# One logarithm over three PSUM banks in a pairwise-attention layer, and 128-column row transforms in a spectral layer

## The chip, the cores and the metric

The kernel runs on one core of one Trainium2 chip, in one launch. A core has five engines that each work through their own queue in order: TensorE (PE in the profile, with its weight loads as PEld), VectorE (DVE), ScalarE (ACT), GpSimd (POOL) and SyncE (SP, which here only issues DMAs). The metric is the device time of one launch in microseconds (us), and lower is better. The kernel before took 3248.14 us (median of 4 runs, 3234.2 to 3256.91).

## The reference

The input x is (4, 32, 128, 128) in float32: four batches of 32 images of 128 x 128 pixels. Two layers follow each other.

Layer 0 is an attention over the 32 images of a batch whose projections are spectral convolutions. Cut to what matters here:

```
x  = x + L0(group_norm(x))
L0: k, q, v = spectral convolutions with 32 heads of the normed images
    p  = spectral convolution of softmax(q k / 64) v;   a = inorm(p + images)
    m  = two spectral convolutions of inorm(a), a gelu between them
    result = inorm(m) + a
spectral convolution: rfft2, keep some modes, multiply by complex weights, irfft2
```

Layer 1 takes each of the four batches as 4096 tokens of 128 channels (32 blocks of 128 tokens). It is an additive attention over all earlier tokens, and a top-2 mixture of 8 experts:

```
f, g   = x W1[:h], x W1[h:]                       # 16 numbers per token
scores = sum_a w2[a] tanh(f_i + g_j + b1)[a] + b2  # for each pair i, j
e      = exp(scores) where j < i, else 0
w      = e / sum(e);   t = t + w x                 # then experts: t = t + sum of the best 2 of 8
```

## The kernel before, in words

**Layer 0.** The two-dimensional transform of an image is two matrix products. `forward` takes eight images at a time (`GI = 8`). In its first half each image, as the stationary operand of TensorE, meets the constant `rows`, whose 192 columns are cos, -sin and -cos of 64 frequencies. Two images fill a PSUM tile `pz` (2 x 192 columns, tag "a", two buffers), and one call of `evacuate` copies it to `z` in SBUF. Over its calls `evacuate` goes round in threes: two go to ScalarE, one to VectorE. In the second half each image of `z` is the stationary operand of two products, with columns 0 to 127 and with columns 64 to 191, which add up in PSUM tile `px` (tag "b"); `take` then reads `px`. A float32 product is two passes in the profile, each with its own weight load. `forward` is called for four groups of eight images by three users in each of four batches: for the images themselves (`spectra_of_images`, tiles named x), for `q` and for `g` (the two calls of `spectra`). That is 48 calls, 384 products into `pz` and 768 passes. `inverse` uses the same tags "a" and "b", and the same `evacuate`. The order of the instructions in layer 0 is made by a scheduler that sees the dependencies.

**Layer 1.** The tanh of a sum is made out of products: `prepare` turns each token into exponentials `qe`, `qf` (as a query) and `ke`, `kf` (as a key) over 2^6, 2^5 and 2^5 sign patterns, so that the score of a pair is a sum over three groups of a numerator `n` over a denominator `d`, each a matrix product with 32 rows to a tile; four such products use different rows of TensorE side by side. The work is cut into 528 units, one for 128 keys by 512 queries (the last of a row is put together out of smaller parts). Each turn `u` of the main loop issues

- `products(u)`: the denominators of unit u and the numerators of unit u - 1, ordered so that both run side by side;
- the logarithm of the denominators on ScalarE, `r = ln(d)`;
- for unit u - 1, whose r is already 1/d, the product n times r on VectorE and two additions on GpSimd that sum the three groups into the score `e`;
- the exponential of -r on ScalarE, in place (which makes 1/d of unit u), and that of the score of unit u - 2;
- `attend(u - 4)`: the product of e with the tokens into `po`.

After these, small pieces of other work, out of lists written by `prepare` and `finish` (norms, transposes, exponentials of keys and queries, the router, the experts `px`), are put in by a rule that counts what each costs. So layer 1's order is fixed by the program (`manual_schedule`). PSUM has eight banks in layer 1, one buffer each: `d0` two, `d1` one, `n0` two, `n1` one, `po` one, and `misc` one. The dictionary `PARTS` says which groups lie in which tile. A tile has to be read before it is written again: the first product of the next unit into `d0` waits for the logarithm of `d0`. After the main loop, `misc` rotates over the freed banks too (list `banks`).

Lines that the text speaks of: `forward` 266 to 283 (products 274, 281 and 282), `evacuate` 215 to 221, `PARTS` 1263, products of the units 1293, logarithm 1346, exp(-r) 1358, exp of the score 1362, product with n 1351, additions 1354 and 1355, `po` 1312, experts 1181 (their sums 1185), `pa` 1121, transposes `pt` 1061, keys and queries 1078 and 1089, router 1159.

Of the kernel before, what the change touches and what calls it, by code (L numbers as in the profile page):

```python
# [7 lines left out]
F32 = mybir.dt.float32  # L8
AF = mybir.ActivationFunctionType
ALU = mybir.AluOpType  # L10
# [3 lines left out]
P = 128  # L14
# [4 lines left out]
GI = 8  # L19
# [16 lines left out]
def _constants():  # L36

    w = np.arange(P)
    kx = np.concatenate([np.arange(32), np.arange(-32, 0)])
    ky = np.arange(KY)  # L40
    th = 2 * np.pi / P
    c, s = np.cos(th * np.outer(w, kx)), np.sin(th * np.outer(w, kx))
    rows = np.concatenate([c, -s, -c], 1)
    inv_rows = np.concatenate([c.T, -s.T], 0)
    angle = th * np.outer(w, ky)
    cc, cs = np.cos(angle), np.sin(angle)

    cols1 = np.concatenate([cc[:, 32:33], cs, cc, -cs], 1) / NPIX
    cols2 = np.concatenate([0 * cc[:, :1], -cc, cs, cc], 1) / NPIX
    twice = np.where(ky == 0, 1.0, 2.0)[:, None]  # L50
    re, im = twice * cc.T, -twice * cs.T
    inv_cols = np.concatenate([re, im], 0)
    p = np.arange(P)
    same = (p[:, None] % 32 == np.arange(32)[None, :]).astype(np.float64)
    block = (p[:, None] // 32 == np.arange(4)[None, :]).astype(np.float64)

    eye = np.eye(32)
    comb = np.zeros((4, 32, 3, 32))
    comb[0, :, 0], comb[3, :, 0] = eye, -eye
    comb[1, :, 1], comb[2, :, 1] = eye, eye  # L60
    comb[:, :, 2] = -comb[:, :, 0]
    halves = np.concatenate([np.eye(64), np.eye(64)], 0)

    group = (p[:, None] // 4 == p[None, :] // 4) / (4.0 * NPIX / C * T)
    of_group = p[:, None] // 4 == np.arange(32)[None, :]
    by_p = np.concatenate(
        [rows, inv_rows, cols1, cols2, same, block, comb.reshape(P, 96), halves, group, of_group / 4],
        1,
    )
    return by_p.astype(np.float32), inv_cols.astype(np.float32)  # L70


NX = 1 + 3 * KY
NCONST = 192 + 128 + 2 * NX + 32 + 4 + 96 + 64 + P + 32
NM = KX * KY
NK = 13

# [27 lines left out]
def layer0(  # L105
    tc, x, kcw, qcw, vcw, pcw, m0cw, m1cw, mcol0, heads, small_row, by_p, inv_cols, dram, x1
):
    nc = tc.nc
    pools = [tc.tile_pool(name="l0_const", bufs=1), tc.tile_pool(name="l0_ps", bufs=2, space=PSUM)]
    pools.append(tc.tile_pool(name="l0_x", bufs=2))  # L110
    const, ps, images = (p.__enter__() for p in pools)
# [17 lines left out]
    def columns(n):  # L129
        at[0] += n  # L130
        return cst[:, at[0] - n : at[0]]

    rows = columns(192)
    inv = columns(128)
    cols1, cols2 = columns(NX), columns(NX)
    same, block = columns(32), columns(4)
# [75 lines left out]

    flip = [0]

    def evacuate(out, in_):

        flip[0] = (flip[0] + 1) % 3
        if flip[0]:
            nc.scalar.copy(out, in_)
        else:  # L220
            nc.vector.tensor_copy(out, in_)

    def per_image(name):
        return small.tile([P, T], F32, name=name, tag=name)
# [41 lines left out]
    def forward(images, c1, c2, take, change=None):  # L266


        n = c1.shape[1]
        z = grp.tile([P, GI, 192], F32, name="z", tag="z")  # L270
        for k in range(0, GI, 2):
            pz = ps.tile([P, 2, 192], F32, name="pz", tag="a")
            for j in range(2):
                nc.tensor.matmul(pz[:, j], images[k + j], rows, start=True, stop=True)  # L274
            evacuate(z[:, k : k + 2], pz)
        if change is not None:
            change(z)
        for k in range(0, GI, 4):
            px = ps.tile([P, 4, n], F32, name="px", tag="b")
            for j in range(4):  # L280
                nc.tensor.matmul(px[:, j], z[:, k + j, :P], c1, start=True, stop=False)  # L281
                nc.tensor.matmul(px[:, j], z[:, k + j, 64:], c2, start=False, stop=True)  # L282
            take(k, px)
# [139 lines left out]
    for part, (a, b, c, d, op) in enumerate(  # L423
# [13 lines left out]
        for y0 in range(0, KA, 16):  # L437
            n = min(16, KA - y0)
# [188 lines left out]
    for b in range(B):  # L627
# [63 lines left out]
        for x0 in range(0, KX, NK):  # L691
# [3 lines left out]
            for i in range(4):  # L695
                xb = late.tile([P, 2, NK * KY], F32, name="xb", tag="xb")[:, :, :m]
                for r in range(2):
                    nc.sync.dma_start(
                        out=xb[:, r],
                        in_=xd[8 * i : 8 * i + 8, r, x0 : x0 + nk]  # L700
# [7 lines left out]
                for k in range(2):  # L708
                    for ri in range(2):
# [6 lines left out]
                        for r in range(2):  # L716
                            j = 2 * ri + r
# [12 lines left out]
        for y0 in range(0, KY, 8):  # L730
            n = min(8, KY - y0)
# [154 lines left out]
        for g in GROUPS:  # L886
            i = slice(g, g + GI)
            for t in range(g, g + GI):
# [5 lines left out]
                    scale=c2[:, t : t + 1],  # L894
# [17 lines left out]
def layer1(tc, x1, w1t_in, signs, vec17, expert_w, expert_b, router_w, small_row, out):  # L912
    nc = tc.nc
# [8 lines left out]
    const, keys, work, small, ps = (p.__enter__() for p in pools)  # L922
# [16 lines left out]
        out=later,  # L939
        in_=later,  # L940
# [15 lines left out]
    banks = ["m"]  # L956

    def misc(name):
# [9 lines left out]
        out=eb.rearrange("p e c -> p (e c)"),  # L968
        in_=expert_b.rearrange("e c -> (e c)").partition_broadcast(P),
    )  # L970
    for w, row in (
# [4 lines left out]
        n = w.shape[1]  # L976
# [283 lines left out]

    PARTS = {"d": (slice(0, 2), slice(2, 3)), "n": (slice(1, 3), slice(0, 1))}

    def two_parts(name):
        return [
# [72 lines left out]
    with tc.manual_schedule():  # L1339
        for u in range(len(units) + 4):  # L1340
            products(u)
            if u < len(units):
                r = work.tile([P, 3, QC], F32, name="r", tag="r", bufs=3)
                live[u, "r"] = r
                for g, d in zip(PARTS["d"], live.pop((u, "d"))):
                    nc.scalar.activation(r[:, g], d, AF.Ln, scale=1.0 / DSCALE)  # L1346
            if 0 <= u - 1 < len(units):
                v = u - 1
                r, n = live.pop((v, "r")), live.pop((v, "n"))
                for g, part in zip(PARTS["n"], n):  # L1350
                    nc.vector.tensor_tensor(r[:, g], part, r[:, g], ALU.mult)  # L1351
                e = work.tile([P, QC], F32, name="e", tag="e", bufs=5)
                live[v, "e"] = e
                nc.gpsimd.tensor_tensor(e, r[:, 1], r[:, 2], ALU.add)  # L1354
                nc.gpsimd.tensor_tensor(e, e, r[:, 0], ALU.add)  # L1355
            if u < len(units):
                r = live[u, "r"]
                nc.scalar.activation(r, r, AF.Exp, scale=-1.0)  # L1358
            if 0 <= u - 2 < len(units):
                c, h, _, parts = units[u - 2]  # L1360
                e = live[u - 2, "e"]
                nc.scalar.activation(e, e, AF.Exp)  # L1362
                if parts[0][0] >= chunks[c][1] + h * QB:

                    width = 2 * P if parts[-1][1] != h else P
                    own = e[:, : len(parts) * width].rearrange("p (k c) -> p k c", c=width)[:, :, :P]
                    nc.gpsimd.tensor_tensor(own, own, later[:, : len(parts)], ALU.mult)  # L1367
            if 0 <= u - 4 < len(units):
                attend(u - 4)
                c, h, is_last, _ = units[u - 4]  # L1370
                if is_last and c == len(chunks) - 1:
                    b, i0 = chunks[c]
                    ending.append((b, i0 + h * QB, QB, [sums[c, h]]))
                elif is_last and h == 1:
                    ending.append((*chunks[c], NB, [sums[c, h] for h in range(2)]))

            if starts and u >= starts[0][0] and not todo:
                _, c, end = starts.pop(0)
                todo = sum(begin(c), [])
            if ending and (not ended or len(ended) == 1 and len(ended[0]) <= 2 * NB):  # L1380
                ended.append(finish(*ending.pop(0)))
            hurry = sum(p[0] in (SOME, LATER) for p in todo) + 6 > end - u
            queues = sorted(ended, key=lambda p: len(p) <= 2 * NB)
            queues.insert(0 if hurry else 2, todo)
            pe, dve, pool = False, 0.0, 0.0
            for pieces in queues:
                while pieces:
                    kind, t_dve, t_pool, piece = pieces[0]
                    if kind == LATER:
                        pieces.pop(0)  # L1390
                        break
                    if kind and pe or dve + t_dve > 1.8 or pool and pool + t_pool > 1.7:
                        break
                    if kind in (SOME, KEEPS) and keeper and keeper[0] is not pieces:
                        break
                    pe, dve, pool = pe or kind > 0, dve + t_dve, pool + t_pool
                    if kind in (KEEPS, KEPT):
                        keeper = [pieces] if kind == KEEPS else []
                    pieces.pop(0)
                    piece()  # L1400
            ended = [p for p in ended if p]

        banks += ["n1", "d1", "n0", "d0"]
        while ended and len(ended[-1]) > 2 * NB:
            ended[0 if len(ended) > 1 and ended[0] else -1].pop(0)[-1]()
        ended.insert(0, finish(*ending.pop(0), last=True))
        while ended:
            for pieces in ended:
                pieces.pop(0)[-1]()
                while pieces and pieces[0][0] in (LATER, KEPT):  # L1410
                    pieces.pop(0)[-1]()
            ended = [p for p in ended if p]
# [69 lines left out]
```

## Time and profile before

| what | value |
|---|---|
| median of 4 runs | 3248.14 us (3234.2 to 3256.91) |
| profiled execution, its own time | 3248.24 us |
| its span in the profile | 3246.4 us |
| mean granted TensorE clock | 0.968 |
| TensorE busy | 2995.8 us (92%) |
| VectorE, ScalarE busy | 2324.0 us and 2327.8 us (72% each) |
| GpSimd busy | 2141.4 us (66%) |
| layer 0 | about 0 to 1160 us |
| layer 1, main loop | about 1160 to 3183 us |
| layer 1, after the loop | about 3183 to 3246 us |

Times in the profile are microseconds from the start of the span. "Idle before, releaser" says how long an engine stood still before a group of instructions, and which instruction's end let it go on. Matmul ends are modelled, and passes overlap, so the distance between the starts of two passes says more than their length.

### The profile page before, as it was taken

To read this page: it belongs to the slowest core of one execution; us is meant where nothing else is said; L and a number is where in the kernel's file an instruction comes from. 1 tells how busy PE (TensorE), PEld (TensorE's weight loads), DVE (VectorE), ACT (ScalarE), POOL (GpSimd) and SP (SyncE) were. 2 spreads that over 40 slices of the span, in tenths; PEclk is the share of its full clock that TensorE was granted. 3 is DMA by queue.
4 is the path that set the end of the run, shared out by engine and by line. 5 is a ranking of instruction groups with operands and counts; after the bars stand their busy time and mean duration, and the time that the engine had idled before them with its cause. 6 is when DMAs were issued, how large, how long until landed. Compare 5 with 4: busy or idle time off the path is not lost.

```text
span 3246.4 us, 53386 instructions
## 1 busy us (share of the span) xinstructions
PE 2995.8 (92%) x19732; PEld 1579.8 (49%) x19732; DVE 2324.0 (72%) x5070; ACT 2327.8 (72%) x3205; POOL 2141.4 (66%) x1883
## 2 busy tenths in 40 slices
PE   6899899899898789999998999998999999999997
PEld 4278458548657634433444444444344434344443
DVE  6776777777676456777765868876677777687787
ACT  2244354354353469999998999998999999899992
POOL 1631551460461259978789887979878889888773
PEclk9899899999999779999999999999999999999998
DMA  4410420330230111010110010011100010101000
GB/s 106 110 34 1 100 71 1 50 121 1 29 116 1 52 47 30 1 37 7 30 37 24 1 36 14 8 30 30 30 16 22 14 36 24 36 1 30 14 14 13
DMA packets 150854, 111.67 MB, mean 34 GB/s; under 512 B 35871, under 2 KB 139394, under 8 KB 149986
## 3 DMA queue, kind: packets, MB, share of 16 engines
q1 hardware_dynamic: 133873, 102.42, 12.6%
q10 hardware_dynamic: 16720, 5.84, 0.8%
q8 instruction: 156, 2.56, 0.3%
q14 instruction: 105, 0.85, 0.1%
HBM read 67.26 MB, written 20.00 MB: 27 GB/s over the span
## 4 chain that ended last, share of the span: by engine, by line
PE 64%; POOL 11%; ACT 9%; DVE 8%; issue 6%; DMA 2%; ACTq 0%; POOLq 0%; DVEq 0%; SPq 0%
PE d L1293 18%; PE po L1312 10%; PE px L1181 6%; ACT r L1346 4%; PE po L718 4%; PE pz L274 4%; PE n L1293 3%; POOL e L1355 3%; PE four L296 3%; POOL e L1354 3%; PE pv L291 3%; PE px L282 2%; PE px L281 2%; ACT e L1362 2%; DVE r L1351 2%
## 5 line engine op out<-in xcount | busy, mean ns | idle before, releaser
L1351 DVE TENSOR_TENSOR r<-n,r 128x1024 f32<-128x1024 f32 (+1 forms) x1056 | 962.0, 953 | 478.6 <-PE n L1293 390.9
L1354 POOL TENSOR_TENSOR e<-r 128x512 f32<-128x512 f32 x528 | 674.0, 1277 | 268.2 <-DVE r L1351 267.5
L1346 ACT ACTIVATE r<-d 128x1024 f32<-128x1024 f32 (+1 forms) x1056 | 793.5, 803 | 64.2 <-PE n L1293 56.7
L1358 ACT ACTIVATE r<-r 128x1536 f32<-128x1536 f32 x528 | 783.5, 1484 | 16.7
L1355 POOL TENSOR_TENSOR e<-e,r 128x512 f32<-128x512 f32 x528 | 672.0, 1273 | 41.4
L1293 PE MATMUL d<-qe,ke 32*128 32x512 f32 (+3 forms) x2304 | 607.8, 602 | 38.2 <-ACT r L1346 36.3
L1312 PE MATMUL po<-e,kx 128*128 128x512 f32 (+3 forms) x1152 | 594.3, 605 | 17.5 <-POOL e L1367 17.5
L1293 PE MATMUL n<-qe,ke 32*128 32x512 f32 (+3 forms) x2304 | 605.2, 601 | 0.0
L1293 PE MATMUL d<-qf,kf 32*128 32x512 f32 (+3 forms) x2304 | 552.4, 554 | 0.0
L1293 PE MATMUL n<-qf,kf 32*128 32x512 f32 (+3 forms) x2304 | 552.2, 554 | 0.0
L1185 DVE SCALAR_TENSOR_TENSOR xc<-px,wgt,xc 128x128 f32<-128x128 f32 x1024 | 358.3, 350 | 43.6 <-PE px L1181 11.1
L1362 ACT ACTIVATE e<-e 128x512 f32<-128x512 f32 x528 | 325.8, 617 | 67.6 <-POOL e L1355 66.6
L1312 PEld LDWEIGHTS po<-e,kx 128*128 128x128 f32 x1152 | 175.4, 188 | 394.2 <-issue 308.7
L1293 PEld LDWEIGHTS d<-qe,ke 32*128 32x128 f32 x2304 | 177.2, 183 | 359.8 <-ACT r L1346 340.7
L800 POOL TENSOR_TENSOR spec<-spec,part 128x264 f32<-128x264 f32 x64 | 55.6, 868 | 391.3 <-DVE part L797 188.7
L713 POOL TENSOR_TENSOR u<-xb,gb 128x858 f32<-128x858 f32 (+1 forms) x120 | 234.7, 1984 | 119.0 <-PE po L718 101.5
L1293 PEld LDWEIGHTS d<-qf,kf 32*128 32x128 f32 x2304 | 220.6, 186 | 176.0 <-issue 163.9
L1181 PE MATMUL px<-we,x2t 128*128 128x512 f32 x512 | 266.5, 607 | 5.6 <-DVE xc L1185 5.5
L715 DVE TENSOR_TENSOR u<-xw,gb 128x858 f32<-128x858 f32 (+1 forms) x200 | 206.0, 1082 | 51.0 <-PE po L718 34.8
L1293 PEld LDWEIGHTS n<-qf,kf 32*128 32x128 f32 x2304 | 227.9, 185 | 19.3 <-issue 12.1
L718 PE MATMUL po<-u,pr 128*32 128x429 f32 (+1 forms) x1280 | 188.8, 541 | 16.6 <-POOL u L713 8.9
L1293 PEld LDWEIGHTS n<-qe,ke 32*128 32x128 f32 x2304 | 177.6, 183 | 9.7 <-DVE r L1351 0.9
(369 smaller groups left out, 4254.8 us busy)
## 6 DMA issues: line engine op xcount, KB each, us to landing
xb<-xd SPq DMA_DIRECT2D x128, 214.5 KB
xc<-x SPq DMA_DIRECT2D x31, 512.0 KB
x<-x SPq DMA_DIRECT2D x16, 512.0 KB
qf<-qe SPq DMA_DIRECT2D x64, 128.0 KB
out<-xc SPq DMA_DIRECT2D x15, 512.0 KB
xb<-xd SPq DMA_DIRECT2D x32, 198.0 KB
gb<-gd SPq DMA_DIRECT2D x4, 1056.0 KB
x<-in_x ACTq DMA_DIRECT2D x8, 512.0 KB
```

Of the source, the lines that this page charges most:

```text
L713: nc.gpsimd.tensor_tensor(u, xb, gk, ALU.mult)
L718: nc.tensor.matmul(po[32 * j : 32 * j + 32], pr[:, i, k], u[:, r], start=i == 0 and k == 0, stop=i == 3 and k == 1,)
L1181: nc.tensor.matmul(px, x2t[:, k * P : (k + 1) * P], we[:, e0 : e0 + 4], start=True, stop=True)
L1185: nc.vector.scalar_tensor_tensor(xc[:, k], px[:, e], wgt[:, k, e0 + e : e0 + e + 1], xc[:, k], ALU.mult, ALU.add)
L1293: nc.tensor.matmul(o, k, q, start=turn == 0 or g > 0, stop=turn == 1 or g > 0)
L1312: nc.tensor.matmul(sums[c, h][:, q0 : q0 + c1 - c0], kx[:, jb], e[:, c0:c1], start=jb == 0, stop=is_last and q0 > 2 * P, skip_group_check= ...
L1346: nc.scalar.activation(r[:, g], d, AF.Ln, scale=1.0 / DSCALE)
L1351: nc.vector.tensor_tensor(r[:, g], part, r[:, g], ALU.mult)
L1354: nc.gpsimd.tensor_tensor(e, r[:, 1], r[:, 2], ALU.add)
L1355: nc.gpsimd.tensor_tensor(e, e, r[:, 0], ALU.add)
L1358: nc.scalar.activation(r, r, AF.Exp, scale=-1.0)
L1362: nc.scalar.activation(e, e, AF.Exp)
```

## The change

It has two parts that do not touch each other.

In layer 1 the three denominators of a unit lie in one PSUM tile `d0` of three banks, where they were in a tile of two and a tile of one. One logarithm of 1536 columns takes the place of one of 1024 and one of 512. The tile's first product of the next unit waits for that one logarithm. After the loop `misc` rotates over four banks (five before), since `d1` is gone.

In layer 0 `rows` has 128 columns (cos and -sin). Four images fill a PSUM tile `pz` of 4 x 128 columns. Two calls of `evacuate` empty it: one copies all 128 columns per image, the other copies the first 64 with the sign changed, and so makes the third block of `z`. To carry the sign, `evacuate` is now an activation with a scale on ScalarE, and a multiplication on VectorE, for all its users. The constant `by_p` is 64 columns narrower.

```diff
-    rows = np.concatenate([c, -s, -c], 1)
+    rows = np.concatenate([c, -s], 1)
...
-NCONST = 192 + 128 + 2 * NX + 32 + 4 + 96 + 64 + P + 32
+NCONST = 128 + 128 + 2 * NX + 32 + 4 + 96 + 64 + P + 32
...
-    rows = columns(192)
+    rows = columns(128)
...
-    def evacuate(out, in_):
+    def evacuate(out, in_, sign=1.0):
 
         flip[0] = (flip[0] + 1) % 3
         if flip[0]:
-            nc.scalar.copy(out, in_)
+            nc.scalar.activation(out, in_, AF.Copy, scale=sign)
         else:
-            nc.vector.tensor_copy(out, in_)
+            nc.vector.tensor_scalar(out, in_, sign, None, ALU.mult)
...
         z = grp.tile([P, GI, 192], F32, name="z", tag="z")
-        for k in range(0, GI, 2):
-            pz = ps.tile([P, 2, 192], F32, name="pz", tag="a")
-            for j in range(2):
+        for k in range(0, GI, 4):
+            pz = ps.tile([P, 4, P], F32, name="pz", tag="a")
+            for j in range(4):
                 nc.tensor.matmul(pz[:, j], images[k + j], rows, start=True, stop=True)
-            evacuate(z[:, k : k + 2], pz)
+
+            evacuate(z[:, k : k + 4, :P], pz)
+            evacuate(z[:, k : k + 4, P:], pz[:, :, :64], -1.0)
...
-    PARTS = {"d": (slice(0, 2), slice(2, 3)), "n": (slice(1, 3), slice(0, 1))}
+    PARTS = {"d": (slice(0, 3),), "n": (slice(1, 3), slice(0, 1))}
...
-        banks += ["n1", "d1", "n0", "d0"]
+        banks += ["n1", "d0", "n0"]
```

## The prediction

> **What bounds the kernel now.** I read the page's busy shares and chain first, then the busy times by stage, then the groups of one layer by shape, and last the single waits.
>
> ```profile
> span 3246.4 us, 53386 instructions
> PE 2995.8 (92%) x19732; PEld 1579.8 (49%) x19732; DVE 2324.0 (72%) x5070; ACT 2327.8 (72%) x3205; POOL 2141.4 (66%) x1883
> PE 64%; POOL 11%; ACT 9%; DVE 8%; issue 6%; DMA 2%; ACTq 0%; POOLq 0%; DVEq 0%; SPq 0%
> ```
>
> TensorE (PE) carries most of the chain. The shares hide two regimes. The next view gives layer 0, layer 1's loop and the tail; behind each window stand its length, then PE, PEld, DVE, ACT, POOL busy, the granted clock, DMA share and GB/s.
>
> ```profile
> 0.00:1160.00 1160.00, 997.33 (x7972) 702.85 (x7972) 802.10 (x1973) 448.33 (x981) 430.58 (x268) 0.93 0.23 56
> 1160.00:3183.00 2023.00, 1954.26 (x11651) 857.18 (x11652) 1473.42 (x2943) 1875.27 (x2215) 1696.49 (x1591) 1.00 0.09 22
> 3183.00:3247.00 64.00, 44.25 (x112) 19.79 (x110) 48.45 (x155) 4.24 (x10) 14.34 (x26) 0.79 0.06 17
> ```
>
> In layer 0 ScalarE (ACT) is busy 448 of 1160 us, so PE and its waits set the pace. In the loop PE, ACT and GpSimd (POOL) are all near full: 97%, 93% and 84% of 2023 us.
>
> Layer 1's groups by shape, and who waits for the logarithm:
>
> ```profile
> L1358 ACT ACTIVATE r<-r 128x1536 f32<-128x1536 f32 x528 | 783.5, 1484 | 16.7
> L1346 ACT ACTIVATE r<-d 128x1024 f32<-128x1024 f32 x528 | 535.9, 1015 | 63.6 <-PE n L1293 56.7 <-PE d L1293 4.8
> L1346 ACT ACTIVATE r<-d 128x512 f32<-128x512 f32 x528 | 311.9, 591 | 0.6 <-PE d L1293 0.6
> ...
>   PEld d L1293: 340.7, 421
> ```
>
> The last line is of those who waited for the logarithm: 421 times a weight load for `d`. Not each such wait costs time, since a weight load may lie beside a running product. One that does, in order of time (start, length, then what):
>
> ```profile
> 1624.71 1.49 ACT L1346 ACTIVATE r<-d 128x1024 f32<-128x1024 f32 x2
> 1625.77 0.70 PE L1293 MATMUL d<-qe,ke 32*128 32x512 f32 x2 [0.34 <-ACT r L1346]
> 1626.24 1.48 ACT L1358 ACTIVATE r<-r 128x1536 f32<-128x1536 f32 x1
> 1627.16 0.59 PE L1293 MATMUL d<-qf,kf 32*128 32x512 f32 x2
> 1627.63 0.61 ACT L1362 ACTIVATE e<-e 128x512 f32<-128x512 f32 x1
> 1628.15 1.49 ACT L1346 ACTIVATE r<-d 128x1024 f32<-128x1024 f32 x2
> ```
>
> ACT starts a pair of logarithms at 1624.71. The first, of 1024 columns, ends near 1625.72; 0.05 us later the products of the next unit start. They overlap the second logarithm, which ends near 1626.2.
>
> Layer 0's groups that count (first two: runs of 8 passes in order of time):
>
> ```profile
> 758.98 1.49 PE L274 MATMUL pz<-cst,q 128*128 128x192 f32 x8
> 214.62 1.06 PE L296 MATMUL four<-icol,v 66*128 66x128 f32 x8
> L219 ACT COPY z<-pz 128x384 f32<-128x384 f32 x127 | 60.7, 478 | 119.9 <-PE pz L274 119.5
> L685 ACT COPY q<-sk 128x512 f32<-128x512 f32 x32 | 18.8, 587 | 39.1 <-PE sk L682 39.0
> L221 DVE COPY z<-pz 128x384 f32<-128x384 f32 x65 | 35.8, 551 | 17.2 <-PE pz L274 16.1 <-issue 0.7
> L794 DVE TENSOR_TENSOR spec<-px,mcw 128x264 f32<-128x264 f32 x64 | 27.6, 431 | 40.0 <-ACT sqx L793 38.7
> ```
>
> **The change, layer 0.** Passes of 192 columns start 162 ns apart (median over the trace; the run of 8 above gives 166). Passes of 128 columns with 128-column weights, as in `four`, start 111 ns apart (112 in the run above). 51 ns x 768 passes = 39 us of PE time, 3.3 us in each of twelve phases of 64 passes. In eight phases (`x` and `g`) DVE is busy some 59 to 77% and PE runs without a break, so I take 24 of 26 us. In the four `q` phases DVE is full (3.87 and 4.00 of 4 us in two stretches there), mostly with sums of line 770 that can wait; I take 4 of 13 us. That makes -28.
>
> Copying stays level. ACT: 478 ns for 384 columns and 587 for 512 make a slope of 0.85 ns a column, so 256 columns take 0.37 us, and a pair of 512 and 256 costs 0.96 us, as two copies of 384 do. VectorE (DVE): 551 for 384, 677 to 679 for 512 (copies of `v`, sums of line 748), so 1.10 us on either side. The instructions stay 192 in number. The scaled form I price like the copy: ACT's square of 132 columns (line 793) takes 281 ns, which lies on the same slope. What is new is order: where one half of a tile goes to ACT and the other to DVE, the second waits for the first, though it needs nothing of it. The trace shows that already: line 794 waits 38.7 us for the square of line 793, which only reads the same tile. Lower bound for this: nothing, and the banks are then waited for less than now (34 us of weight loads waited for copies, some 25 us of it felt by PE). Upper bound: each of 96 tiles is held up by 0.42 us (256 columns on DVE), +40 us, all of the gain. I take no net effect, as the 16 passes of `px` (16 x 2 x 0.111 = 3.6 us) lie between a group's copies and their use and cover 1.1 us three times. If DVE's queue is late, that cover is gone; this is the third case below. Layer 0: -28, from -45 to 0. The narrower constant, 32 KB less in one DMA at the start, I set at nothing: the images' DMAs land beside it.
>
> **Layer 1.** From the start of the pair to exp(-r) it takes 1.53 to 1.54 us (1624.71 to 1626.24). A logarithm of 1536 columns, by the slope from 591 to 1015 ns, takes 1.44 to 1.46 us; with the 0.03 us before exp(-r) this is 1.49. ACT saves 0.05 us a unit, 28 us over 528 if ACT were the only bound. Against that, the first product of the next `d` starts 0.44 us later relative to the logarithm's start (1.46 in place of 1.02).
>
> The Trainium skill puts both sides in one place (Perfetto Trace Analysis, Optimizing Scalar/DVE Operations). It says that larger operations help where the engine is saturated, at some 51 ns saved for each on PSUM, and that where it is not saturated but makes others wait, splitting helps. The first half agrees with our 0.05 us and would make the sum -27 us here; the second half speaks against the change, and would make it a loss.
>
> Which of the two decides differs by interval. I measured all 527 from one unit's first `d` product to the next's. 229 contain two expert passes and take 3.84 us, set by PE; there `d` starts 0.31 us after the second logarithm's end, so nothing changes. 102 contain no other product; there `d` starts 0.43 us before the second logarithm ends. The loop then is 1.98 us of `d`, 0.02, a logarithm of 1.46 and 0.05, thus 3.51, where most take 3.43 now (set by ACT) and some 3.09. Walking the trace with that rule (`d` starts at the later of PE being free and the logarithm's end + 0.05; the logarithm at the later of the end of `d` and ACT being free, each ACT turn 0.05 shorter) gives +16 us for these 102, +4 for 62 with `pa`, +3 for 58 with transposes, +1 for the rest: +24. About 5 of it fall where POOL never pauses, in the stretches at 4.15 us a unit, and are lost in its queue. I take +19. Bounds: if ACT alone decided, -6 (the walk with the 0.05 alone); if every early start was pushed back and nothing absorbed it, 102 x 0.43 + 60 x 0.24 + 51 x 0.23 + 67 x 0.22 = +85. The value lies near the walk, since it follows both chains; I trust it from +8 to +37.
>
> **The tail.** Four banks in turn in place of five. DVE is busy 48 of 64 us there and takes 1.4 us for an expert tile that PE makes in 0.9, so PE only loses run-ahead: nothing, at most +2.
>
> Sum: -28 + 19 = -9. The profiled execution took 3248.24 us (span 3246.4 and 1.8 around it), 0.1 from the median. Forecast 3239 us.
>
> **Rivals.** (1) Both parts as summed, between -16 and +16 us (0.5% of the time, about what a measurement here can tell from no change), thus 3232 to 3264: 0.44. (2) Faster: layer 0 gives all 39 and 6 of the bank waits, POOL absorbs layer 1 down to 10: -35, 3213 us. For it speaks that every `pz` pass is on the chain; against it the full DVE in `q`. 0.31. (3) Slower, in `forward`: the second copy of a tile waits behind other work in DVE's queue, ACT behind it stands still, and `px` starts late. It decides from 0.26 us a tile ((28 - 19 + 16) / 96); at 0.42 it makes +31, 3279 us. For it speaks line 794's wait, against it the cover of 3.6 us. 0.14. (4) Slower, in layer 1: the later `d` is not absorbed. At the bound of +85 this is 3305 us. Against it: 229 intervals have 0.31 us to spare. 0.06. (5) The passes do not shrink, as the weight load bounds them: +19, 3267 us. `four` speaks against it. 0.05.
>
> So faster 0.31, same 0.44, slower 0.25. The range runs from case 2 to case 3, without the ends of each: 3210 to 3272.
>
> **What would show it.** `pz` passes 111 ns apart; no waits of `px` for `z`; layer 0 ending 25 to 30 us earlier. In layer 1 one logarithm near 1.46 us; intervals without other products at 3.5 us; expert intervals still 3.84; the loop 15 to 25 us longer. Wrong if layer 0 ends less than 12 us earlier, or if the loop grows by more than 37 us or not at all.

## The result, and the profile after

The change made the kernel very slightly slower. The forecast was 9 us faster.

| what | before | after |
|---|---|---|
| median | 3247.32 us (56 runs) | 3253.05 us (35 runs) |
| ratio after / before, 95% interval | | 1.0018 [1.0010, 1.0027], that is +5.8 us [3.2, 8.8] |
| profiled execution, span | 3248.24, 3246.4 us | 3250.45, 3248.4 us |
| mean granted TensorE clock | 0.968 | 0.963 |
| first product of `d` (end of layer 0) | 1158.3 us | 1143.9 us |
| from the first product of `d` to the last | 2022.3 us | 2039.3 us |

The last two rows say where to look: in the profiled pair layer 0 is 14.4 us shorter, where 28 were forecast, and layer 1's loop is 17.0 us longer, where 19 were forecast.

The page of the kernel after, span, busy times and shares of the chain:

```profile
span 3248.4 us, 52888 instructions
PE 2943.7 (91%) x19732; PEld 1515.1 (47%) x19732; DVE 2324.0 (72%) x5070; ACT 2310.1 (71%) x2677; POOL 2140.8 (66%) x1883
PE 57%; POOL 11%; ACT 11%; DVE 7%; issue 4%; DMA 1%; SPq 0%; POOLq 0%; DVEq 0%; ACTq 0%
```

TensorE has 52 us less work, and the time did not follow: its share of the chain fell from 64 to 57%, and ScalarE's rose from 9 to 11%. The same by stage (layer 0, the loop, the tail; behind each window its length, then PE, PEld, DVE, ACT and POOL busy, granted clock, DMA share, GB/s):

```profile
0.00:1146.00 1146.00, 963.52 (x7973) 671.11 (x7973) 800.16 (x1973) 444.99 (x981) 430.16 (x268) 0.91 0.23 57
1146.00:3185.00 2039.00, 1937.66 (x11648) 826.23 (x11648) 1474.97 (x2942) 1860.24 (x1686) 1695.78 (x1590) 0.99 0.09 22
3185.00:3249.00 64.00, 42.51 (x114) 17.77 (x112) 48.92 (x156) 4.82 (x11) 14.88 (x27) 0.87 0.06 17
```

Layer 0 lost 34 us of PE's busy time and 14 us of its length, so some 20 us came back as idle PE. The loop is longer with all three of its engines a little less busy: a wait grew. The tail kept its 64 us.

**Layer 1.** The first products of `d` in the kernel before, by shape; then the merged logarithm and the same products after; then two units of the kernel after in order of time, at about the place that the prediction showed:

```profile
L1293 PE MATMUL d<-qe,ke 32*128 32x512 f32 x1920 | 544.0, 641 | 33.6 <-ACT r L1346 32.0
```

```profile
L1348 ACT ACTIVATE r<-d 128x1536 f32<-128x1536 f32 x528 | 764.6, 1448 | 97.4 <-PE n L1295 78.9 <-PE d L1295 10.8
L1295 PE MATMUL d<-qe,ke 32*128 32x512 f32 x1920 | 545.9, 643 | 67.4 <-ACT r L1348 62.5
```

```profile
1622.56 1.45 ACT L1348 ACTIVATE r<-d 128x1536 f32<-128x1536 f32 x1
1624.05 1.48 ACT L1360 ACTIVATE r<-r 128x1536 f32<-128x1536 f32 x1
1624.07 0.70 PE L1295 MATMUL d<-qe,ke 32*128 32x512 f32 x2 [0.48 <-ACT r L1348]
1625.03 0.59 PE L1295 MATMUL d<-qf,kf 32*128 32x512 f32 x2
1626.10 1.45 ACT L1348 ACTIVATE r<-d 128x1536 f32<-128x1536 f32 x1
1627.60 0.70 PE L1295 MATMUL d<-qe,ke 32*128 32x512 f32 x2 [0.48 <-ACT r L1348]
```

The merged logarithm takes 1.448 us. The next unit's `d` starts 0.06 us after its end, and not beside a second logarithm as before; from the start of the logarithm to that product it is 1.51 us, where it was 1.06 (1624.71 to 1625.77 before). In the two units shown a turn takes 3.54 us (1622.56 to 1626.10), where the one that the prediction showed took 3.44. The wait of these `d` products for the logarithm doubled, from 32.0 to 62.5 us.

**Layer 0.** The passes into `pz` now start 112 ns apart (median; 163 before), and ScalarE and VectorE take the mixed copies at about the durations that were worked out:

```profile
L274 PE MATMUL pz<-cst,q 128*128 128x128 f32 x256 | 31.8, 276 | 0.0
L219 ACT ACTIVATE z<-pz 128x512 f32<-128x512 f32 x63 | 37.6, 596 | 75.9 <-PE pz L274 74.6 <-issue 1.3
L219 ACT ACTIVATE z<-pz 128x256 f32<-128x256 f32 x64 | 24.3, 379 | 27.2 <-DVE z L221 27.1
L221 DVE TENSOR_SCALAR z<-pz 128x512 f32<-128x512 f32 x33 | 22.5, 683 | 4.2 <-PE pz L274 3.5 <-issue 0.7
L283 PE MATMUL px<-cst,z 128*128 128x99 f32 x512 | 101.5, 281 | 4.7 <-ACT z L219 2.4 <-DVE z L221 0.9 <-DVE n_r_ve L238 0.5
L283 PE MATMUL px<-colg,z 128*128 128x67 f32 x256 | 49.4, 278 | 3.3 <-DVE z L476 3.0 <-DVE rm_t L242 0.3
```

Where the gain went is seen by following batch 0. Measured from the first to the last pass of a phase, the twelve phases with `pz` became 38.9 us shorter in sum (x 14.9, q 13.7, g 10.3). But in batch 0 the first product with the values (`po`) starts 8.5 us later than before (136.3 against 127.8), although the x phase ahead of it ended 6.4 us earlier (64.1 against 70.5). That alone is 14.9 us. The DMA queue of SP, before and then after (start, length from first to last issue, what):

```profile
68.46 0.33 SPq L517 DMA_DIRECT2D gd<-g  x1
76.22 5.13 SPq L487 DMA_DIRECT2D xd<-xx  x2
81.86 2.80 SPq L519 DMA_DIRECT2D gb<-gd  x2
87.30 16.15 SPq L698 DMA_DIRECT2D xb<-xd  x5
```

```profile
73.44 10.33 SPq L489 DMA_DIRECT2D xd<-xx  x2
83.86 3.25 SPq L519 DMA_DIRECT2D gd<-g  x1
93.52 1.27 SPq L521 DMA_DIRECT2D gb<-gd  x2
94.90 14.75 SPq L700 DMA_DIRECT2D xb<-xd  x5
```

`gd` is a store to DRAM that belongs to the values' weights (`value_weights`), and `gb` loads the same data back, spread over the partitions. Before, the second store of `gd` was issued at 68.46, ahead of the two stores of `xd`. After, it stands behind them, at 83.86. The loads of `gb` wait for the store, and the ten loads of `xb` stand behind `gb` in the queue: they start at 94.90 and not at 87.30. ScalarE's timeline shows who pays, before and then after:

```profile
109.28 0.52 ACT L707 COPY xw<-xb 128x429 f32<-128x429 f32 x1 [30.09 <-DMA xb<-xd]
110.81 0.58 ACT L573 COPY spt<-sp 128x512 f32<-128x512 f32 x1
```

```profile
117.21 0.52 ACT L709 COPY xw<-xb 128x429 f32<-128x429 f32 x1 [40.80 <-DMA xb<-xd]
119.26 0.58 ACT L575 COPY spt<-sp 128x512 f32<-128x512 f32 x1
```

The copy of `xb` waits for its DMA, and the copy `spt` of the scores is queued behind it on ScalarE, though its data have been there since the score products ended (106.5 before, 103.8 after). On PE the next product needs `spt` (before, after):

```profile
111.45 1.91 PE L584 MATMUL sc<-spt,cst 128*32 128x512 f32 x2 [4.97 <-ACT spt L573]
```

```profile
119.89 1.91 PE L586 MATMUL sc<-spt,cst 128*32 128x512 f32 x2 [16.14 <-ACT spt L575]
```

PE's wait is 11 us longer. Nothing in the diff names `gd`: the scheduler of layer 0, which was given other instructions to order, put the store elsewhere. SP's order is the same in `l0_only` (below), which has the same layer 0, so it belongs to the program and not to one execution.

### The profile page after: what moved, and what is told of

Same layout as the page of the kernel before. It is cut to its first block, busy times and chain, and to the rows that moved or that the text cites. A ratio compares the mean times of both kernels' runs of the same rounds, so it can differ in the third digit from the quotient of the medians.

```text
span 3248.4 us, 52888 instructions
## 1 busy us (share of the span) xinstructions
PE 2943.7 (91%) x19732; PEld 1515.1 (47%) x19732; DVE 2324.0 (72%) x5070; ACT 2310.1 (71%) x2677; POOL 2140.8 (66%) x1883
## 4 chain that ended last, share of the span: by engine, by line
PE 57%; POOL 11%; ACT 11%; DVE 7%; issue 4%; DMA 1%; SPq 0%; POOLq 0%; DVEq 0%; ACTq 0%
PE d L1295 22%; PE po L1314 9%; ACT r L1348 7%; PE px L1183 5%; POOL e L1357 3%; POOL e L1356 3%; PE po L720 3%; PE n L1295 2%; PE four L298 2%; PE pv L293 2%; PE px L284 2%; PE px L283 2%; PE pz L274 1%; POOL kx L1048 1%; DVE xc L1187 1%
## 5 line engine op out<-in xcount | busy, mean ns | idle before, releaser
L1348 ACT ACTIVATE r<-d 128x1536 f32<-128x1536 f32 x528 | 764.6, 1448 | 97.4 <-PE n L1295 78.9
L1295 PEld LDWEIGHTS n<-qf,kf 32*128 32x128 f32 x2304 | 219.9, 186 | 6.5 <-issue 0.2
L709 ACT COPY xw<-xb 128x429 f32<-128x429 f32 (+1 forms) x160 | 83.9, 528 | 137.2 <-DVE pa L561 64.9
```

The lines of the kernel that those rows point to most:

```text
L1295: nc.tensor.matmul(o, k, q, start=turn == 0 or g > 0, stop=turn == 1 or g > 0)
```

## The experiments

Three theories stood against each other. Queue: layer 0's passes gave what was forecast, and SP's new order took part of it back. Layer 1: the later `d` costs more than 19 us. Copies: the second copy of a tile holds ScalarE up (the third rival). All ratios are to the kernel before on the same chip, with the 95% interval in microseconds; 6 to 12 runs of each build.

**The parts alone.** `l1_only` has only layer 1's part:

```diff
-    PARTS = {"d": (slice(0, 2), slice(2, 3)), "n": (slice(1, 3), slice(0, 1))}
+    PARTS = {"d": (slice(0, 3),), "n": (slice(1, 3), slice(0, 1))}
...
-        banks += ["n1", "d1", "n0", "d0"]
+        banks += ["n1", "d0", "n0"]
```

> Only layer 1's part of the change is made: one tile d0 of three banks, one logarithm of 1536 columns, four banks in the tail; layer 0 is that of before. Theory A (the next unit's denominators start 0.44 us later, and nothing covers it where no other product stands in between): the loop grows by 15 us, as it did between the two profiles (2020.3 to 2035.6 us from the first logarithm to the last product), so +13 to +19 us, a ratio of 1.004 to 1.006. Rival B (ScalarE is the bound and gains 0.05 us in each of 528 units): -6 us or less. Rival C (the units absorb the later start, and the change's loss comes from layer 0): within 3 us of before.

Measured: 3264.6 us, ratio 1.0042 [1.0026, 1.0058], +13.6 us [8, 19]. The loop is 2038.9 us, as in the kernel after. `l0_only` has the rest of the change, without these lines.

> Only layer 0's part is made: 128 columns, two copies per tile of four images; layer 1 is that of before. Theory A (the twelve phases gain about 35 us, but the scheduler's new order gives part back: in the first batch the second store of gd stands behind the stores of xd in SyncE's queue, and all that follows starts later): layer 1 begins 14 us earlier, as between the two profiles, so -9 to -15 us. Rival B (the passes save 39 us and the order costs nothing): -28 us or more. Rival C (copies of a tile by two engines in turn eat the gain in the phases): the phases of 64 passes shrink by less than 1.5 us each, total within 5 us of before.

Measured: 3238.35 us, ratio 0.9963 [0.9950, 0.9976], -12.0 us [-16, -8]; loop 2022.7 us. So layer 1 costs no more than the 19 that were forecast, and layer 0 gives less than half of its 28 us. The sum of the two, +1.6 us, agrees with the +5.8 of the whole change within the intervals. This speaks against the layer 1 theory and leaves layer 0 to explain.

**The order of the queue, first try.** `l0_vw_first` is `l0_only` with the values' weights built ahead of the x phase of batch 0, so that `gd` stands early in SP's queue; `vw_first` is its control, the same move in the kernel before.

```diff
+    value_weights()
     front = spectra_of_images(0, loaded, normed)
-    value_weights()
```

> As l0_only, but the weights of the values (the two stores of gd and the loads of gb) are issued in the program ahead of the first images' spectra, so the second store of gd stands ahead of xd in SyncE's queue, as in the kernel before. Theory A: the first po of batch 0 starts near 125 us and not 136 us, and the gain is 20 to 25 us against before, some 10 us more than l0_only. Rival C (the copies eat the gain, the order of the queue does not matter): the same time as l0_only within 3 us.

> Control: the kernel before with the weights of the values issued ahead of the first images' spectra, and nothing else changed. Theory A: the order of the queue was good already, so within 3 us of before. If it is faster by as much as l0_vw_first is against l0_only, the move helps by itself, and theory A's reading of the first batch is wrong.

Measured: `l0_vw_first` 3230.21 us, 0.9938 [0.9921, 0.9956], -20 us [-26, -14]; `vw_first` 3254.55 us, 1.0010 [0.9998, 1.0022], +3 us [-1, +7]. The move helps the changed layer 0 by 8 us and does not help the kernel before, as the queue theory says. It is not a clean repair: the x phase of batch 0 became longer (34.5 us instead of 21.8), so the first `po` came at 130.2 us and not at 125.

**Both parts with this move**, `after_vw_first`:

> Both parts of the change, with the weights of the values issued ahead of the first images' spectra. Theory A (the parts do not touch each other, and the order of SyncE's queue is worth some 8 us): -20 and +13.6 add up to -6 us, so -2 to -11 us against before; that is the sign that was predicted. Rival C (order is worth nothing): +2 to +6 us, as the whole change has.

Measured: 3253.95 us, 1.0011 [0.9999, 1.0022], +3.6 us [0, +7]. This missed: in the kernel after the move is worth 2 us (+5.8 to +3.6), and the two parts would give -6.5 us, each by its own medians. In the profile layer 0 ends at 1153.5 us here and at 1137.1 in `l0_vw_first`, although layer 0 has the same instructions in the same order in both; single profiles of the same layer 0 differ by such amounts elsewhere too (`l0_only` 1154.1, the kernel after 1143.9). So the profiled pair alone can't settle 10 us of layer 0, and the medians must. What makes the difference between these two builds stays open, so the queue theory rests on the second try.

**The order of the queue, second try.** `l0_gd_act` is `l0_only` with only the second store of `gd` and its two loads moved from SP's queue to ScalarE's. In the traces the instructions of VectorE and GpSimd before layer 1 stand in the same order as in `l0_only`, SP lacks only these three DMAs, ScalarE has them beside one exchange of neighbours in a later batch, and starts on PE differ by at most four places.

```diff
-            nc.sync.dma_start(out=gd[ri], in_=g.rearrange("n x y -> n (x y)"))
+            eng = nc.scalar if ri else nc.sync
+            eng.dma_start(out=gd[ri], in_=g.rearrange("n x y -> n (x y)"))
             for k in range(2):
-                nc.sync.dma_start(
+                eng.dma_start(
```

> As l0_only, but the second store of gd and the two loads of gb behind it are issued by ScalarE, so that SyncE's queue goes from xd straight to xb. Theory A (the queue holds up the first batch): the first po starts at 128 us or before, and the time is 8 to 12 us under l0_only, -20 to -24 us against before. Rival D (it is not the queue but the late weights themselves, which VectorE makes later in the new order): the first po stays near 136 us and the time is that of l0_only.

Measured: 3228.78 us, 0.9934 [0.9914, 0.9954], -21 us [-28, -15]. SP's queue and ScalarE in this build:

```profile
74.31 10.40 SPq L489 DMA_DIRECT2D xd<-xx  x2
90.68 21.79 SPq L701 DMA_DIRECT2D xb<-xd  x9
```

```profile
106.22 0.52 ACT L710 COPY xw<-xb 128x429 f32<-128x429 f32 x1 [28.94 <-DMA xb<-xd]
110.25 0.58 ACT L576 COPY spt<-sp 128x512 f32<-128x512 f32 x1
```

`xb` starts 4.2 us earlier than in the kernel after, `spt` 9.0 us earlier (110.25 against 119.26), and the first `po` comes at 127.1 us. So the start of `xb` explains about half. The rest lies between that start and the first copy of `xb`: 22.3 us in the kernel after (94.90 to 117.21), where the two `gb` loads of 1056 KB each were issued just ahead, and 15.5 us here. That these loads slowed `xb` was not tested apart. The next two put the same edit into the kernel after and, as a control, into the kernel before.

> The changed kernel with the second store of the gate's spectra and its two loads issued from ACT's queue instead of SP's. Theory A (the parts add up: layer 0 with this order is worth -20 us as measured without layer 1's part, layer 1's part costs +13.6): -2 to -11 us against the kernel before, and the first matmul against the values near 127 us instead of 136.3. Theory B (layer 0's gain does not carry over when layer 1's part is present, as the run with the value weights first suggests at +3.6): 0 to +6 us, with the first such matmul early all the same.

> Control: the kernel before with only that store and its loads on ACT's queue. There the store already stands ahead of the loads of the x spectra on SP (68.46 against 76.22), so theory A (the move repairs only what the change had put out of order) expects no change, within 3 us, and the first matmul against the values between 125 and 129 us. Theory B (the move is worth its 9 us in any kernel): 7 to 12 us faster.

Measured: `after_gd_act` 3243.45 us, 0.9985 [0.9971, 0.9999], -4.9 us [-9, 0], first `po` at 124.2; `gd_act` 3249.44 us, 0.9997 [0.9985, 1.0009], -1.0 us [-5, +3], first `po` at 124.2 (125 to 129 expected for `gd_act`). The times are those of theory A in each expectation. The edit is worth 9 us in `l0_only` (-12.0 to -21.4), 11 us in the kernel after (+5.8 to -4.9), both with an uncertainty of 5 to 8 us, and nothing clear in the kernel before, where the store was early already. With it, the kernel after is faster than before, by some 5 us. That this is near the forecast of 9 is partly luck: layer 0 gives some 20 us in place of 28, and layer 1 costs 13.6 in place of 19.

These two builds show one thing more. With the same edit, the first `po` starts at 124.2 us in both, although the x phase of batch 0 ends at 64.0 us with the new passes and at 72.0 with the old ones. In this pair the shorter x phase of batch 0 brings nothing.

**How much a later `d` costs.** `l1_swap` is the kernel before with the two logarithms issued in the other order, that of 512 columns first. Nothing is merged, so ScalarE saves nothing, and the bank pair that the next `d` needs first is read last.

```diff
-                for g, d in zip(PARTS["d"], live.pop((u, "d"))):
+                for g, d in list(zip(PARTS["d"], live.pop((u, "d"))))[::-1]:
```

> The kernel before with its two tiles and two logarithms, but the one of 512 columns (d1) goes first and the one of 1024 (d0) second. ScalarE's work is that of before; only d0, which the next unit's first products need, comes free 0.49 us later. Theory A (the late release is what layer 1 pays for): the walk over the intervals gives +35 us, of which about a quarter falls where GpSimd is the bound, so +18 to +30 us, and more than l1_only, whose one logarithm is also 0.05 us shorter. Rival B (the form of the logarithm over three banks is what costs, not when it ends): within 4 us of before.

Measured: 3283.32 us, 1.0105 [1.0088, 1.0122], +34 us [29, 40]; loop 2054.4 us, +32. ScalarE and PE in this build:

```profile
1636.28 1.51 ACT L1346 ACTIVATE r<-d 128x512 f32<-128x512 f32 x2
1637.83 1.48 ACT L1358 ACTIVATE r<-r 128x1536 f32<-128x1536 f32 x1
1639.90 1.51 ACT L1346 ACTIVATE r<-d 128x512 f32<-128x512 f32 x2
```

```profile
1637.85 0.70 PE L1293 MATMUL d<-qe,ke 32*128 32x512 f32 x2 [0.57 <-ACT r L1346]
1641.47 0.70 PE L1293 MATMUL d<-qe,ke 32*128 32x512 f32 x2 [0.57 <-ACT r L1346]
```

A turn takes 3.62 us here. The first `d` product starts 1.57 us after the start of the pair (1.51 with the merged logarithm, 1.06 before), and this costs 34 us with nothing merged. So a late release is enough to cause layer 1's loss. The merged logarithm, which lets both the next `d` and exp(-r) start 0.06 us sooner than this, costs some 20 us less. It cost more than expected (18 to 30); the walk alone gave 35, so what I had taken off for GpSimd was too much here.

**The additions on GpSimd.** In batch 2 the score products (`sp`) took 33.6 us after and 28.6 before, and in the kernel after each of the four additions x + g stands between two `pb` products of GpSimd that `sp` waits for. GpSimd before, and after, at that place:

```profile
592.05 2.35 POOL L896 TENSOR_TENSOR x<-x,g 128x1024 f32<-128x1024 f32 x1 [23.50 <-ACT g L889]
595.13 2.36 POOL L896 TENSOR_TENSOR x<-x,g 128x1024 f32<-128x1024 f32 x1 [0.73 <-ACT g L889]
599.85 3.78 POOL L561 TENSOR_TENSOR pb<-xm 128x1024 f32<-128x1024 f32 x2 [2.36 <-ACT xm L495]
```

```profile
591.72 1.91 POOL L563 TENSOR_TENSOR pb<-xm 128x1024 f32<-128x1024 f32 x1 [27.38 <-ACT xm L497]
595.07 2.36 POOL L898 TENSOR_TENSOR x<-x,g 128x1024 f32<-128x1024 f32 x1 [1.44 <-ACT g L891]
597.39 1.91 POOL L563 TENSOR_TENSOR pb<-xm 128x1024 f32<-128x1024 f32 x1
599.26 2.36 POOL L898 TENSOR_TENSOR x<-x,g 128x1024 f32<-128x1024 f32 x1
```

Three builds move these additions to VectorE: `l0_vw_add_dve` in `l0_vw_first`, `add_dve` in the kernel before, and `l0_gd_add_dve` in `l0_gd_act`.

```diff
-            nc.gpsimd.tensor_tensor(xr[:, i], xr[:, i], gl[:, i], ALU.add)
+            nc.vector.tensor_tensor(xr[:, i], xr[:, i], gl[:, i], ALU.add)
```

> As l0_vw_first, but the four additions of x and g per batch (128x1024) go to VectorE, so GpSimd runs its twelve products pb of a batch without additions in between. Theory A (in the third batch's score products sp, 33.5 us long with 128 columns and 28.6 before, the scheduler put all four additions among the products where two were): that stretch shrinks to 29 us or less and the total by 4 to 8 us against l0_vw_first, if VectorE can hide 4 x 1.1 us per batch behind sp; rival: VectorE's additions delay the last products and the total does not change.

> Control: the kernel before with only the additions x+g moved from POOL to DVE. Score products of batches 1 to 3 take 30.8, 28.6 and 31.8 us there, 24.6 with the additions on DVE in the other build. Theory A (POOL holds the score products back in the kernel before as well): 3 to 10 us faster, score products 24 to 26 us. Theory B (the move repairs only batch 2, where the change put all four additions in the products): within 3 us.

> Layer 0 in 128 columns, the second gate store and its loads on ACT's queue, the additions x+g on DVE, layer 1 as before. If the two repairs add up (-21 for the queue, another 5 for the additions): 24 to 28 us faster than before, the best of the builds; if both free the same stretch: 19 to 23.

Measured:

| build | median us | ratio [95%] | us to before |
|---|---|---|---|
| `l0_vw_add_dve` | 3224.99 | 0.9925 [0.9905, 0.9946] | -24 |
| `add_dve` | 3239.36 | 0.9960 [0.9945, 0.9976] | -13 |
| `l0_gd_add_dve` | 3217.64 | 0.9899 [0.9881, 0.9918] | -33 |

The score products of batches 1 to 3 take 24.5 to 24.7 us in all three. `l0_vw_add_dve` gains 4 us over `l0_vw_first`, and `l0_gd_add_dve` 11 us over `l0_gd_act`, more than expected (24 to 28 us under before). But the gain is there in the kernel before too, with 13 us even larger than the 3 to 10 expected: GpSimd held the score products back all along, so this is an improvement beside the change and not a repair of it. In the profiled pair the four score stretches became 3.9 us longer in sum (batch 2 longer by 5.0, batch 3 shorter by 2.6); by the medians the move is worth no more with the new layer 0 than without it. `l0_gd_add_dve`, layer 0 in 128 columns with both edits and layer 1 as before, is the fastest of the builds: 1.0% under the kernel before.

## Why the prediction was wrong

The forecast was 3239 us, from -28 for layer 0 and +19 for layer 1. The time was 3253, inside the range, and within 0.5% of the kernel before, the case that had got the largest chance (0.44); but the sign of the central number was wrong. The term that failed is layer 0's -28: it came out at -12.0 us [-16, -8]. Step by step:

- *51 ns for each of 768 passes, 39 us.* Right: 163 to 112 ns, and 38.9 us shorter phases in the profiled pair (36.0 in `l0_only`). They are not alike: g of batch 1 became 1.7 us longer, the others 2.5 to 5.8 shorter. And a shorter phase is not yet a shorter launch; that is the step that failed, below.
- *The q phases take only 4 of 13 us, because VectorE is full.* Wrong by 10 us for the phases: they became 13.7 us shorter. VectorE's load there could wait, as the prediction itself said of line 770. The x and g phases became 25.2 us shorter, for the 24 that were taken.
- *The copies stay level, under the cover of the 16 passes of `px`.* Level in sum, but not by the cover. The copies of 512 columns took 596 and 683 ns (587 and 677 to 679 estimated). The wait of the second copy exists (ScalarE waited 27.1 us in all for VectorE's half, 15 times), and products of `px` did wait for `z`: 7.3 us in all, 0.9 before, 3.0 of it for the correction in line 476 of the kernel after, which follows the copies. "No waits of `px` for `z`" did not come true. Against that, products of `pz` waited 4.7 us for their bank, 10.1 before. In sum this is 12.0 us after and 11.0 before, so the third rival, which needed 25 us, did not come.
- *The narrower constant costs nothing.* Nothing speaks against it: the first pass starts at 42.39 us (42.84 before).
- *What an earlier end of a phase starts.* This is the step that failed. The -28 let each phase's gain reach the end of layer 0. It counted batch 0 as elsewhere ("PE runs without a break"), had no term for the order of the DMA queue, and named only the constant's DMA. Three things stood in its place.
  - The order of SP's queue. The loads of `xb` came to stand behind the store and loads of `gd`, and the first `po` behind them started 8.5 us later. The price is 9 to 11 us, shown by moving that one store and its loads and by the control.
  - The x phase of batch 0 was hidden to begin with. The chain between 60 and 140 us of the kernel before has the DMA of `xb` at 23.6% and of `xd` at 18.1%, ahead of every line of PE there; and with the same edit in both kernels the first `po` starts at 124.2 us, whichever passes the x phase has.
  - Behind the first `po` a part is lost as well. From there to the first `d`, five profiles with the old passes take 1026.8 to 1039.4 us (mean 1033) and six with the new ones 1006.9 to 1019.0 (mean 1013; the builds with the additions on VectorE left out). That is 20 us less, while the phases in this stretch are some 31 us shorter. Two pieces that grew in all six are the score products of batch 2 (29.2 to 29.6 us before, 34.1 to 34.2 after) and the time between the q and the g phase of batch 3 (25.8 to 29.8 before, 30.2 to 34.4 after). Why was not tested.

  With the queue mended layer 0 is worth -21 us [-28, -15], against -28 forecast.
- *One logarithm near 1.46 us, `d` 0.05 after its end, the loop without other products at 3.51 us.* Right: 1.448, 0.05 to 0.06 and 3.54. Units with two expert passes still take 3.84.
- *+16 for the 102 intervals with no other product, +4 with `pa`, +3 with transposes.* In the profiled pair these groups grew by 20.1, 5.0 and 0.0 us; their median intervals went from 3.43 to 3.54, from 3.46 to 3.54, and stayed near 3.54. Those with expert passes, which were to keep their time, shrank by 9.1 us in sum at an unchanged median, so the walk's total of +24, of which 5 were taken off, was too high by some 7. All intervals together grew by 17.0 us.
- *+19 for layer 1.* Right in sign and mechanism, at the upper end of what was measured: the loop grew by 17.0 us, and alone the part costs +13.6 us [8, 19].
- *The tail takes nothing.* Right: 64 us again.

The bound given for being wrong, a layer 0 that ends less than 12 us earlier, lies where layer 0 came out: 14.4 us in the profiled pair, 12.0 us by the medians of `l0_only`. A bound so close to what one profile of layer 0 scatters by should have been put on the medians.

The Trainium skill (Perfetto Trace Analysis, Optimizing Scalar/DVE Operations) has grouping for a saturated engine, and splitting for one that is not saturated but keeps others waiting. ScalarE is busy 93% of the loop before, so neither condition is met cleanly, and both effects are seen here in one place: the merged logarithm starts exp(-r) 0.04 to 0.05 us sooner a unit, and the part as a whole costs +13.6 us [8, 19], because TensorE waits for the banks.

## What to carry to other kernels

Where a scheduler orders the instructions, a shorter phase also moves what stands around it: read the DMA queue of the changed program line by line in the stretches that are bound by transfers, above all a store that other loads wait for, and ask what is queued behind those loads. Of a logarithm or a copy that frees a PSUM bank, ask when it ends as well as how long it takes; merging two of them delays the first release, and where the other engine waits for that bank the merge can lose more than the saved overhead. A gain in a stretch that ends in a DMA is no gain until that DMA starts earlier.

## What the runs showed that was not expected

- Three DMAs on another queue were worth 9 to 11 us of 3250, with the same bytes moved in both builds (264 KB by the store, 1056 KB by each load): the queue that they stood in decided.
- Moving four additions of 2.36 us a batch from GpSimd to VectorE made the kernel before 13.0 us faster [8, 18], although VectorE is the busier engine in layer 0 (802 of 1160 us against 431 for GpSimd).
- The granted clock was lower where PE had gaps. Over the score products of batch 2 it is 0.74 in the kernel after, with PE busy 74% of the time, and 0.93 in the build with the additions on VectorE, with PE busy 95% and about the same work. Two windows show that they go together, and not which causes which. The windows, after and then `l0_gd_add_dve`:

```profile
594.00:627.00 33.00, 24.41 (x130) 4.55 (x132) 24.20 (x21) 10.55 (x28) 29.95 (x15) 0.74 0.37 60
```

```profile
584.00:608.50 24.50, 23.39 (x134) 4.29 (x132) 24.50 (x22) 10.97 (x29) 20.76 (x12) 0.93 0.53 81
```

- Layer 0's end scatters by some 10 us between single profiles of the same layer 0, while layer 1's loop repeats within 3 us (2020.7 to 2023.3 us over the nine kernels with the loop as before).
